# A recurrent attention layer with a sign-weight feed-forward gate on one core: where the dots of a block are summed, and where the last block's output weights are requested

## The chip, the cores and the metric

The kernel runs on one core of a Trainium2 chip. The metric is the device time of one execution in microseconds (us). The core has five engines that each work through their own instructions in order: PE (TensorE, matmuls), DVE (VectorE), ACT (ScalarE), POOL (GpSimd) and SP (SyncE). Here SP issues the plain transfers, and POOL issues those that add to what lies at the target. PSUM is the memory that TensorE writes; the kernel holds six rotating banks for matmul results ("mm") and one bank each for two running sums ("dots" and "squares").

## The reference, cut to what matters

All numbers are float32. x has 2048 tokens of 512 values. There are 16 heads of 128 channels, so 2048 channels.

```python
xn = layernorm(x)
q, k, v = (silu(xn @ W) for W in (Wq, Wk, Wv))     # 512 -> 2048 channels
z, a, b = xn @ Wz, xn @ Wa, xn @ Wb                # a, b: one value per head
q, k, v = (causal_dwconv4(u, w) for u, w in ...)   # 4 taps over the tokens
q, k = rotate(q), rotate(k); q, k = q / |q|, k / |k|    # per head
for s in range(4):                                  # lags 0..3
    attn = sum_over_head(q * lag(k, s)) / sqrt(128)
    out += attn * sigmoid(lag(a, s) * b) * lag(v, s)
out = out * rsqrt(mean(out * out)) * norm_w * silu(z)
s = out @ Wout                                      # 2048 -> 512
g = silu((relu(xn @ sign(up)) * up_scale) @ sign(down) * down_scale * output_scale)
return x + s * g
```

The "dots" are the sums of q times lagged k over each head's channels, for four lags: 16 heads x 4 lags x 2048 tokens.

## The kernel before, in words

**Blocks and pairs.** The tokens are worked on in four blocks of 512 (b = 0 to 3), and the channels in eight pairs of heads (p = 0 to 7), 256 channels each, which lie as two halves (j = 0, 1) of 128 partitions. `step(p, b)` (line 563) does for one pair the q and k work of block b+1 and the v, z and output work of block b, so that the block behind and the block ahead are interleaved. Steps with b = -1 do only the q and k work of block 0, with the feed-forward of block 0 between (lines 695 to 713). Steps with b = 0, 1, 2 follow (715 to 717), and after them a loop written out for the last block's v, z and output work (719 to 781). From line 789 on comes the feed-forward of blocks 1 to 3.

**q and k.** `queries` and `products` project a pair (eight matmuls of 128x512 each for q and k), convolve on ACT and DVE, and rotate (`turn`). `products` then multiplies q with lagged k on DVE: a tile `pr` of 128x2048 for half 0 and `pr1` for half 1, from a pool tag "pr" with two buffers. The halves have to be added. In block 0 (`not b`) DVE adds pr1 to pr for pairs 0 to 5, and an accumulating transfer of POOL does it for pairs 6 and 7 (lines 362 to 365). In the other blocks POOL does it for even pairs; an odd pair is formed with DVE adds and then gathered by four POOL transfers of 32 partitions into the tile of the even pair before it (lines 376 to 383), so that one tile holds two pairs.

**Dots.** An entry in `dots_due` says which tile has to be summed over partitions. `sum_dots` (line 405) takes one entry and issues four matmuls with a 32-column stationary (the trace shows each matmul of fp32 operands as two records, so eight records), one per lag, into the bank "dots". In blocks 1 to 3 there are four entries per block, each summed in the step two pairs later. In steps with p = 2, 4 and 6 `sum_dots` stands after the v projection and ahead of the output projection (lines 586 and 587); with p = 0 it is handed to `output_projections` as `midway`, which calls it after two of four chunks (lines 532 and 593).

**Norms and coefficients.** `sum_squares` sums q and k squares into the bank "squares"; `norms` copies half of them with ACT (line 432, the tile shares tag "rk" with the staging tile of `gate_products`, line 228, from which POOL sums into ab_dram), takes the root on ACT and the reciprocal on DVE. `coefficients` (line 453) multiplies dots, norms and gates and stores 128x512 coefficients to DRAM (co_dram).

**v, z and output.** `values` convolves v. `weighted` (line 484) loads the coefficient rows of a pair, spread over 64 partitions each, as tiles `bc` (two per pair, four transfers, three buffers), and forms o on DVE. `gated_output` multiplies o by norm_w and silu(z) into `oz`. After each odd pair `output_projection` (line 529) multiplies oz of two pairs with wo: four chunks `po` of 128 tokens, four matmuls each (32 records in all). The first matmuls of a chunk need the even pair's oz and wo, the others the odd pair's. ACT copies each po to `part`, and POOL adds it to s_dram.

**Weights.** `load` (line 250) requests 512 KB of wq, wk, wv or wz into a pool with three buffers. `weights_of_output` (line 471) requests wz and then wo (three buffers of its own) of a pair; `gates_of_output` (line 477) projects z.

**What sets the order.** TensorE, DVE and some POOL instructions keep the order in which the program is written (class `InOrder`, line 68). ACT, the other POOL instructions and SP are ordered by a scheduler from dependencies and priorities; SP's requests in the last block are kept in written order from line 720 on. A request whose buffer is not yet free waits at the head of SP's queue, and all later requests wait behind it.

**The last block.** Lines 721 to 732 request v of pairs 0 and 1 and z and wo of pair 0, finish norms and dots, and form the coefficients. In the loop from line 752, iteration p requests z and wo of pair p (`zs`, line 761), v of pair p+2 (line 764), and then, in `weighted` (line 769), the bc rows of pair p:

```python
        if 0 < p < NP:
            zs = weights_of_output(p, last)
            v = values(p, last, raw)
        if p + 2 < NP:
            load(vs, "v", p + 2, last)
```

Of the kernel before, what the change touches and what calls it, by code (L numbers as in the profile page):

```python
# [49 lines left out]
LAGS = 4  # L50
# [3 lines left out]
NP = H // 2  # L54
# [27 lines left out]
def recurrent_layer(ctx: ExitStack, tc: tile.TileContext, a: dict, out: bass.AP):  # L82
    nc = tc.nc
# [3 lines left out]
    loads = {"by": nc.sync}  # L87
# [5 lines left out]
    of_head = const.tile([P, NP, LW], F32, name="of_head")  # L93
# [3 lines left out]
    of_heads = const.tile([P, NP // 2, LW], F32, name="of_heads")  # L97
# [150 lines left out]
    weights = {}  # L248

    def load(pool, n, p, b):  # L250
        w = pool.tile([P, KC, 2 * P], F32, tag="w", name=f"w{n}{p}_{b}", bufs=3)
        loads["by"].dma_start(w, a[f"w{n}"][p])
        weights[n] = w
# [24 lines left out]
    def raw_of(pool, n, p, b, bufs=2):  # L278

        raw = with_halo(pool, f"r{n}", "raw", bufs, p, b)  # L280
        project(n, p, b, raw[:, :, HALO:])
        keep_halo(f"r{n}", raw, p, b)
        return raw
# [15 lines left out]
    banks = {}  # L299

    dots_due = []
# [26 lines left out]
    def products(p, b, q, between=None, beside_k=None):  # L328

        n = f"_{p}_{b}"  # L330
        load(qks, "k", p, b)
        q0 = q[:, LAGS - 1]
        k = with_halo(qks, "k", "k", 1, p, b)
        raw = raw_of(qks, "k", p, b)
        if p % 2 == 0:
            sum_squares()
        convolve(1, p, raw, k[:, :, HALO:])
        keep_halo("k", k, p, b)
        if between:
            between()  # L340
        turn(q)
        if beside_k:
            beside_k()

        sq = [qks.tile([P, 2, TB], F32, tag=f"sq{j}", name=f"sq{j}" + n, bufs=2 - j) for j in range(2)]
        for j in range(2):
            nc.scalar.activation(sq[j][:, 0], q0[:, j], AF.Square)
            nc.scalar.activation(sq[j][:, 1], k[:, j, HALO:], AF.Square)
        nc.gpsimd.dma_start(sq[0], sq[1], accum_op=ALU.add)
        squares_due.append((p, sq[0]))  # L350
        def product(to, j, lo, hi):

            k0 = k[:, j, lo : lo + TB]
            k_lags = bass.AP(k0.tensor, k0.offset, [k0.ap[0], [1, hi - lo], k0.ap[1]])
            dve.tensor_tensor(to, q[:, lo:hi, j, :], k_lags, ALU.mult)

        pr = qks.tile([P, LAGS, TB], F32, tag="pr", name="pr0" + n, bufs=2)
        product(pr, 0, 0, LAGS)
        if not b or p % 2 == 0:
            pr1 = qks.tile([P, LAGS, TB], F32, tag="pr", name="pr1" + n, bufs=2)  # L360
            product(pr1, 1, 0, LAGS)
            if b or p >= NP - 2:
                nc.gpsimd.dma_start(pr, pr1, accum_op=ALU.add)
            else:
                dve.tensor_tensor(pr, pr, pr1, ALU.add)
        else:
            for lo in range(0, LAGS, 2):
                half = qks.tile([P, 2, TB], F32, tag="half", name=f"half{lo}" + n, bufs=1)
                product(half, 1, lo, lo + 2)
                dve.tensor_tensor(pr[:, lo : lo + 2], pr[:, lo : lo + 2], half, ALU.add)  # L370
        if not b:
            dots_due.append([p, pr, of_head[:, p], p == NP - 1, True])
            return


        for h in range(0, P, D // 2):
            first, second = slice(h, h + D // 4), slice(h + D // 4, h + D // 2)
            if p % 2 == 0:
                nc.gpsimd.dma_start(pr[first], pr[second], accum_op=ALU.add)
            else:  # L380
                both = dots_due[-1][1]
                nc.gpsimd.dma_start(both[second], pr[first])
                nc.gpsimd.dma_start(both[second], pr[second], accum_op=ALU.add)
        if p % 2 == 0:
            dots_due.append([p, pr, of_heads[:, p // 2], p == NP - 2, False])
        else:
            dots_due[-1][-1] = True

    def add(to, s, heads, src, start, stop):

        rows = to[LW * s : LW * s + LW, :]
        pe.matmul(rows, heads, src, start=start, stop=stop, tile_position=(0, LW * s))
# [11 lines left out]

    def sum_dots():

        p, pr, heads, last, _ = dots_due.pop(0)
        if p == 0:
            banks["dots"] = sums.tile([P, TB], F32, tag="dots", name="dots")
        for s in range(LAGS):  # L410
            add(banks["dots"], s, heads, pr[:, LAGS - 1 - s, :], p == 0, last)

    def sums_of_o(b):

# [49 lines left out]
    def values(p, b, raw):  # L464

        v = with_halo(vs, "v", "v", 1, p, b)
        convolve(2, p, raw, v[:, :, HALO:])
        keep_halo("v", v, p, b)
        return v

    def weights_of_output(p, b):
        load(vs, "z", p, b)
        wo = vs.tile([P, 2, HID], F32, tag="wo", name=f"wo_{p}_{b}", bufs=3)
        nc.sync.dma_start(wo, a["wo"][p])
        return weights["z"], wo

    def gates_of_output(p, b, loaded=None):

        weights["z"], wo = loaded or weights_of_output(p, b)
        z = vs.tile([P, 2, TB], F32, tag="z", name=f"z_{p}_{b}", bufs=1)  # L480
        project("z", p, b, z)
        return z, wo

    def weighted(p, b, v):

# [67 lines left out]
    def output_projections(midway=None):  # L553
        if midway and not outputs_due:
            midway()
        while outputs_due:
            outputs_due.pop(0)(midway)
            midway = None
# [4 lines left out]
    def step(p, b, beside_q=None, beside_k=None):  # L563

        at = b >= 0
        change = p == 0 and at
        q = queries(p, b + 1)
        if beside_q:
            beside_q()
        if change and b:  # L570
            sum_squares()
            norms(b)
        due = bool(dots_due) and dots_due[0][-1]
        if change and not b:

            def beside_k():
                norms(b)
                norms_in_rows(b)

        products(p, b + 1, q, (lambda: norms_in_rows(b)) if change and b else None, beside_k)  # L580
        if p == NP - 1 and b + 2 < NTB:
            gate_products(b + 2)
        if at:
            load(vs, "v", p, b)
            raw = raw_of(vs, "v", p, b, 1)
        if due and not change:
            sum_dots()
        if first_due:
            first_due.pop()()
        if at:  # L590
            v = values(p, b, raw)

        output_projections(sum_dots if change else None)
        if change:
            coefficients(b)
        if at:
            z, wo = gates_of_output(p, b)
            out_of = lambda: gated_output(p, b, weighted(p, b, v), z, wo)
            if change:
                first_due.append(out_of)  # L600
            else:
                out_of()
        if p == 1 and at:
            gate(b + 1)
        if b + 2 < NTB:
            if p < TC:
                statistics(b + 2, p)
            if p == TC - 1:
                centre(b + 2)
            elif p == 5:  # L610
                divide(b + 2)
# [102 lines left out]
    vs = att.enter_context(tc.tile_pool(name="vs", bufs=1, side="right"))  # L714
# [4 lines left out]
    last = NTB - 1  # L719
# [1 line left out]
    load(vs, "v", 0, last)  # L721
    raw = raw_of(vs, "v", 0, last, 1)
    load(vs, "v", 1, last)
    zs = weights_of_output(0, last)
    sum_squares()
    norms(last)
    norms_in_rows(last)
    v = values(0, last, raw)
    raw = raw_of(vs, "v", 1, last, 1)
    sum_dots()  # L730
    coefficients(last)
    output_projections()
# [19 lines left out]
    for p in range(NP + 1):  # L752
        if 1 < p < NP:
            weights["v"] = v_weights.pop(p)
            raw = raw_of(vs, "v", p, last, 1)
        if p:
            z, wo = gates_of_output(p - 1, last, zs)
        if p % 2 == 1:
            output_projections()
        if 0 < p < NP:  # L760
            zs = weights_of_output(p, last)
            v = values(p, last, raw)
        if p + 2 < NP:
            load(vs, "v", p + 2, last)
            v_weights[p + 2] = weights["v"]
        if p:
            gated_output(p - 1, last, o, z, wo)
        if p < NP:
            o = weighted(p, last, v)

        if p < NP:
            some = slice(2 * p, 2 * p + 2)
            pool.dma_start(up[:, some], signs_dram["up"][:, some])
        else:
            pool.dma_start(first_down, signs_dram["down"][:, 0:NFD])
        if p == 4:
            xs = in_two_terms(ffw, tokens(1), "xs", 1, [P, KC, TB], "xs1")
# [11 lines left out]
    with tc.tile_pool(name="ff", bufs=1, side="right") as ff, tc.tile_pool(  # L789
# [48 lines left out]
        for b in range(1, NTB):  # L838
            pf = [pfs.tile([P, HID], F32, name=f"pf{c}") for c in range(TC)]
            for f in range(2, NFC + 2):  # L840
# [19 lines left out]
                _, df, terms = hids.pop(0)  # L860
# [88 lines left out]
```

## Time and profile before

| what | value |
|---|---|
| time, median of 3 runs | 1442.33 us (1441.13 to 1446.36) |
| time of the profiled execution | 1443.7 us |
| its span, first to last instruction | 1441.9 us |
| mean granted TensorE clock | 0.992 |
| TensorE busy | 1408.2 us, 98% of the span |
| DVE busy | 1207.8 us, 84% |
| ACT busy | 611.4 us, 42% |
| HBM read and written | 157.67 and 35.68 MB |

A row of the waits gives who waited (engine, tile), for what, the total in us, how often, and the longest. A row of a timeline gives start and length in us, engine, line, operation, output and inputs, the number of records, and in brackets the idle time before it with what ended it. Nearly all TensorE, DVE and SP work shows line 76, the wrapper that keeps the written order, so rows are told apart by their tiles: pq, pk, pv, pz are projections, po the output projection, dots the sums. In the answers of the chain a line gives start, length and what worked or was waited for.

### The profile page before, as it was taken

The page shows a single profiled execution, that of the slowest core. Times are in us where ns is not written, and L with a number is a line of the kernel's source. Part 1 is how long each engine was busy: PE and PEld are TensorE (multiplying, and loading weights), DVE is VectorE, ACT ScalarE, POOL GpSimd, SP SyncE. Part 2 cuts the span into 40 slices and gives each one's busy share as a digit, 9 for nine tenths or more (in the row PEclk, how much of TensorE's full clock was granted, in tenths as well). Part 3 has the DMA queues.
Part 4 walks back from the last instruction along what each step waited for, and adds up shares of the span by engine and source line. Part 5 has one row for each costly group of instructions (what it writes and reads, how often), then busy time and mean ns, then how long its engine had stood idle before and what let it go on. Part 6 is the DMA issues. An engine that isn't in the chain of part 4 may idle for free. (4 is left out here: it accounts for less than half of the span.)

```text
span 1441.9 us, 12588 instructions
## 1 busy us (share of the span) xinstructions
PE 1408.2 (98%) x3950; PEld 686.5 (48%) x3950; DVE 1207.8 (84%) x1362; ACT 611.4 (42%) x1181; POOL 232.4 (16%) x319
## 2 busy tenths in 40 slices
PE   9999998999999999999999999999999999799998
PEld 4555543444434444444344444444443444378886
DVE  6999988999999979999999799999896777346454
ACT  7476555444444534454444435444432332132122
POOL 2222121111212121212122201121211111100000
PEclk9999999999999999999999999999999999899999
DMA  9879598887988687878986888796749777662120
GB/s 330 253 192 214 138 234 189 222 209 178 203 199 191 137 194 223 202 179 194 212 193 137 190 211 199 169 216 169 166 94 230 198 196 170 149 223 93 35 88 29
DMA packets 102065, 261.30 MB, mean 181 GB/s; under 512 B 18864, under 2 KB 19376, under 8 KB 97392
## 3 DMA queue, kind: packets, MB, share of 16 engines
q0 software_dynamic: 33376, 106.99, 38.4%
q1 hardware_dynamic: 68624, 153.53, 35.4%
q8 instruction: 31, 0.51, 0.1%
q14 instruction: 34, 0.28, 0.1%
HBM read 157.67 MB, written 35.68 MB: 134 GB/s over the span
## 5 line engine op out<-in xcount | busy, mean ns | idle before, releaser
L76 PE MATMUL po<-wo,oz 128*128 128x512 f32 x512 | 230.5, 607 | 9.4 <-DVE oz L76 9.4
L76 PE MATMUL pv<-xnT,wv 128*128 128x512 f32 x512 | 226.5, 594 | 2.2 <-DMA wv<-in_wv_dram 2.2
L76 PE MATMUL pz<-xnT,wz 128*128 128x512 f32 x512 | 226.1, 594 | 0.7 <-DMA wz<-in_wz_dram 0.7
L76 PE MATMUL pq<-xnT,wq 128*128 128x512 f32 x512 | 226.0, 593 | 0.2 <-ACT xnT L177 0.2
L76 PE MATMUL pk<-xnT,wk 128*128 128x512 f32 x512 | 225.2, 592 | 0.0
L76 PEld LDWEIGHTS po<-wo,oz 128*128 128x128 f32 x512 | 97.9, 194 | 141.6 <-issue 109.7
L76 DVE SCALAR_TENSOR_TENSOR q<-rq,conv_w,q 128x512 f32<-128x512 f32 x192 | 141.4, 749 | 27.8 <-ACT q L288 23.2
L76 DVE SCALAR_TENSOR_TENSOR k<-rk,conv_w,k 128x512 f32<-128x512 f32 x192 | 142.3, 751 | 23.5 <-ACT k L288 19.0
L76 PEld LDWEIGHTS pv<-xnT,wv 128*128 128x128 f32 x512 | 95.6, 189 | 130.2 <-issue 121.6
L76 PEld LDWEIGHTS pz<-xnT,wz 128*128 128x128 f32 x512 | 96.7, 190 | 126.5 <-issue 123.6
L76 PEld LDWEIGHTS pq<-xnT,wq 128*128 128x128 f32 x512 | 96.0, 189 | 126.1 <-issue 118.5
L76 PEld LDWEIGHTS pk<-xnT,wk 128*128 128x128 f32 x512 | 96.6, 189 | 121.0 <-issue 115.6
L76 DVE SCALAR_TENSOR_TENSOR v<-rv,conv_w,v 128x512 f32<-128x512 f32 x192 | 141.3, 750 | 4.5
L76 DVE SCALAR_TENSOR_TENSOR q<-q,turns 128x1024 f32<-128x1024 f32 (+1 forms) x128 | 127.1, 1014 | 2.3
L76 DVE TENSOR_TENSOR o<-o,te 128x1024 f32<-128x1024 f32 x96 | 117.6, 1225 | 3.3
L76 DVE TENSOR_TENSOR pr<-q,k 128x2048 f32<-128x2048 f32 x52 | 117.3, 2287 | 0.9
L76 DVE TENSOR_TENSOR te<-v,bc 128x1024 f32<-128x1024 f32 x96 | 117.0, 1219 | 0.4 <-DMA bc<-co_dram 0.4
L647 ACT ACTIVATE hid<-ph,up_scale 128x512 f32<-128x512 f32 x64 | 43.7, 684 | 120.0 <-PE ph L76 118.8
L76 DVE CAST hid_hi<-hid 128x512 fp32r<-128x512 f32 x64 | 27.2, 425 | 69.9 <-ACT hid L647 69.9
L76 PE MATMUL ph<-xs_hi,up 128*128 128x512 f32 x192 | 76.4, 398 | 0.7 <-ACT so_sb L419 0.7
L276 ACT ACTIVATE rq<-pq 128x512 f32<-128x512 f32 x64 | 38.1, 595 | 90.7 <-PE pq L76 90.6
L76 PE MATMUL ph<-xs_lo,up 128*128 128x512 f32 x192 | 75.8, 395 | 0.0
(142 smaller groups left out, 1660.0 us busy)
## 6 DMA issues: line engine op xcount, KB each, us to landing
bc<-co_dram SPq DMA_DIRECT2D x128, 256.0 KB, 6.4
pr<-pr POOLq DMA_DIRECT2D x72, 256.0 KB, 5.9
wq<-in_wq_dram SPq DMA_DIRECT2D x32, 512.0 KB, 6.4
wk<-in_wk_dram SPq DMA_DIRECT2D x32, 512.0 KB, 6.2
sq<-sq POOLq DMA_DIRECT2D x32, 512.0 KB, 6.3
wv<-in_wv_dram SPq DMA_DIRECT2D x32, 512.0 KB, 6.5
wz<-in_wz_dram SPq DMA_DIRECT2D x32, 512.0 KB, 6.3
wo<-in_wo_dram SPq DMA_DIRECT2D x32, 512.0 KB, 6.0
```

The source lines that it names most:

```text
L76: return self.tc.keep_in_program_order(getattr(self.engine, op)(*args, **kwargs))
L276: nc.scalar.activation(to[:, j, :], pp, AF.Silu)
L647: nc.scalar.activation(hid, ph, AF.Relu, scale=up_scale[:, f : f + 1])
```

## The change

In block 0 DVE adds the halves of pair 6 too, and the halves of pair 7 are not added at all: `dots_due` now holds a list of tiles, and `sum_dots` goes through pr and pr1 of pair 7 with four matmuls each, all into the same bank. In the steps with p = 2, 4 and 6 `sum_dots` is handed to `output_projections` as `midway`, as it was with p = 0. In the last block wo is requested on its own (`load_wo`), after the bc rows of the same pair, and wo of pair 0 behind wv of pair 2, both ahead of the coefficient store.

```diff
-            if b or p >= NP - 2:
+            if b:
                 nc.gpsimd.dma_start(pr, pr1, accum_op=ALU.add)
-            else:
+            elif p < NP - 1:
                 dve.tensor_tensor(pr, pr, pr1, ALU.add)
...
-            dots_due.append([p, pr, of_head[:, p], p == NP - 1, True])
+            prs = [pr, pr1] if p == NP - 1 else [pr]
+            dots_due.append([p, prs, of_head[:, p], p == NP - 1, True])
...
-        for s in range(LAGS):
-            add(banks["dots"], s, heads, pr[:, LAGS - 1 - s, :], p == 0, last)
+        for pr in prs:
+            for s in range(LAGS):
+                src = pr[:, LAGS - 1 - s, :]
+                add(banks["dots"], s, heads, src, p == 0, last and pr is prs[-1])
...
-    def weights_of_output(p, b):
-        load(vs, "z", p, b)
+    def load_wo(p, b):
         wo = vs.tile([P, 2, HID], F32, tag="wo", name=f"wo_{p}_{b}", bufs=3)
-        nc.sync.dma_start(wo, a["wo"][p])
-        return weights["z"], wo
+        loads["by"].dma_start(wo, a["wo"][p])
+        return wo
...
-        if due and not change:
-            sum_dots()
         if first_due:
             first_due.pop()()
...
-        output_projections(sum_dots if change else None)
+        output_projections(sum_dots if due else None)
...
     load(vs, "v", 1, last)
-    zs = weights_of_output(0, last)
+    load(vs, "z", 0, last)
     sum_squares()
...
     raw = raw_of(vs, "v", 1, last, 1)
+    load(vs, "v", 2, last)
+    wo = load_wo(0, last)
     sum_dots()
     coefficients(last)
...
         if 0 < p < NP:
-            zs = weights_of_output(p, last)
+            load(vs, "z", p, last)
             v = values(p, last, raw)
+        if p and p + 2 < NP:
+            load(vs, "v", p + 2, last)
         if p + 2 < NP:
-            load(vs, "v", p + 2, last)
             v_weights[p + 2] = weights["v"]
...
             o = weighted(p, last, v)
+        if 0 < p < NP:
+            wo = load_wo(p, last)
```

In the steps, `gates_of_output` now only projects z; the requests of wz and wo stand in front of it in `step` in the same order as before.

More of the change, by code (lines that the diff above doesn't have):

```diff
@@ L380, in products @@
             else:
-                both = dots_due[-1][1]
+                both = dots_due[-1][1][0]
                 nc.gpsimd.dma_start(both[second], pr[first])
@@ L384, in products @@
         if p % 2 == 0:
-            dots_due.append([p, pr, of_heads[:, p // 2], p == NP - 2, False])
+            dots_due.append([p, [pr], of_heads[:, p // 2], p == NP - 2, False])
         else:
@@ L405, in sum_dots @@
     def sum_dots():
-        p, pr, heads, last, _ = dots_due.pop(0)
+        p, prs, heads, last, _ = dots_due.pop(0)
         if p == 0:
             banks["dots"] = sums.tile([P, TB], F32, tag="dots", name="dots")
-        for s in range(LAGS):
-            add(banks["dots"], s, heads, pr[:, LAGS - 1 - s, :], p == 0, last)
+        for pr in prs:
+            for s in range(LAGS):
+                src = pr[:, LAGS - 1 - s, :]
+                add(banks["dots"], s, heads, src, p == 0, last and pr is prs[-1])
     def sums_of_o(b):
@@ L469, in values, with gates_of_output @@
         return v
-    def weights_of_output(p, b):
-        load(vs, "z", p, b)
+    def load_wo(p, b):
         wo = vs.tile([P, 2, HID], F32, tag="wo", name=f"wo_{p}_{b}", bufs=3)
-        nc.sync.dma_start(wo, a["wo"][p])
-        return weights["z"], wo
-    def gates_of_output(p, b, loaded=None):
-        weights["z"], wo = loaded or weights_of_output(p, b)
+        loads["by"].dma_start(wo, a["wo"][p])
+        return wo
+    def gates_of_output(p, b):
         z = vs.tile([P, 2, TB], F32, tag="z", name=f"z_{p}_{b}", bufs=1)
         project("z", p, b, z)
-        return z, wo
+        return z
     def weighted(p, b, v):
@@ L596, in step @@
         if at:
-            z, wo = gates_of_output(p, b)
+            load(vs, "z", p, b)
+            wo = load_wo(p, b)
+            z = gates_of_output(p, b)
             out_of = lambda: gated_output(p, b, weighted(p, b, v), z, wo)
@@ L756, in recurrent_layer @@
         if p:
-            z, wo = gates_of_output(p - 1, last, zs)
+            z = gates_of_output(p - 1, last)
         if p % 2 == 1:
```

## The prediction

> **What bounds the kernel now.** I read the page's busy shares first, then TensorE's waits, then the timeline at each wait, then the chain that ended last.
>
> ```profile
> PE 1408.2 (98%) x3950; PEld 686.5 (48%) x3950; DVE 1207.8 (84%) x1362; ACT 611.4 (42%) x1181; POOL 232.4 (16%) x319
> ...
> PE po L76 <- DVE oz L76: 9.4, 5, 7.7
> PE dots L76 <- DMA pr<-pr: 7.6, 2, 4.3
> PE dots L76 <- issue: 3.2, 1, 3.2
> PE pv L76 <- DMA wv<-in_wv_dram: 2.2, 1, 2.2
> ```
>
> TensorE is busy for 98% and waits for about 27 us in all (total, times, longest). So only its waits and its pace can be won. Three of them are dots waiting for a sum of pr; the longest is po waiting for oz.
>
> ```profile
> 221.40 1.93 PE L76 MATMUL dots<-pr,of_head 128*32 128x512 f32 x8 [4.29 <-DMA pr<-pr]
> ...
> 283.48 12.28 PE L76 MATMUL po<-wo,oz 128*128 128x512 f32 x28 [0.28 <-DVE oz L76]
> ...
> 426.31 1.93 PE L76 MATMUL dots<-pr,of_heads 128*32 128x512 f32 x8 [3.34 <-DMA pr<-pr]
> 428.17 14.57 PE L76 MATMUL po<-wo,oz 128*128 128x512 f32 x32
> ...
> 575.91 12.28 PE L76 MATMUL po<-wo,oz 128*128 128x512 f32 x28 [0.68 <-DVE oz L76]
> ...
> 718.55 1.07 PE L76 MATMUL dots<-pr,of_heads 128*32 128x512 f32 x8 [3.15 <-issue]
> 719.56 15.64 PE L76 MATMUL po<-wo,oz 128*128 128x512 f32 x32
> ```
>
> TensorE's timeline at the places that the change touches (start, us, idle before). The wait at 718.55 is put down to "issue", but it stands where the one at 426 stood a block earlier and the instruction waits for the same four pr transfers, so I take it as the same wait. After each wait the pace is low for a while: 32 records of po take 13.74 elsewhere, 15.64 here.
>
> ```profile
> 1208.58 12.03 PE po L76 x28
> ...
> 1220.63 0.33 SPq L474
> ...
> 1222.03 10.86 DMA bc<-co_dram
> ...
> 1242.33 15.37 PE po L76 x28
> ```
>
> The chain in the last block: wo of pair 7 (L474) waits on SP until po of pair 5 has freed its buffer, the bc rows of pair 7 stand behind it, o starts when they land, and TensorE idles 7.70 us; the 28 records after it take 15.37 for 12.03.
>
> [...] 3.15 to 4.29 us of idling cost 1.6 to 1.9 more, 7.70 cost 3.3, 2.23 (at 1094) none. [...] from 200 to 216 us, with ten weight loads on SP, the DMA share is 1.00 and POOL's small ab_dram sums take 6 us each.
>
> **Part 1, first block's pairs 6 and 7.** Removed: two 1 MB accumulating transfers (median 9.4 us). Added: one DVE add of 128x2048 for pair 6, 2.29 us (its row at 158.64), and four more matmuls for pair 7, 8 records, 1.0 us on TensorE. The add is hidden by DVE's waits for ACT up to 204.6 (0.79, 0.70, 0.79, together 2.28); uncovered it would cost 2.3. TensorE reaches dots at 217.1, the second product of pair 7 is done at 203.8, so the 4.29 wait goes, with 1.6 of slow pace (dots 1.93 for 1.06, then 7.60 for 6.87), less 1.0: TensorE is 4.9 us ahead at pq (226.0 for 230.86).
>
> It meets oz of pair 1 next, which let it go on at 283.48 (wait 0.28). DVE has run since 222.67 with only two waits, for ACT's k multiply (0.71 and 1.21), and these go with an earlier pk: -1.9. Against that, in the built order of the changed kernel ACT's copy of the squares stands ahead of the second k multiply, no longer behind it:
>
> ```profile
> 211.36 0.72 ACT L288 ACTIVATE k<-rk,conv_w 128x512 f32<-128x512 f32 x1
> 215.63 0.58 ACT L432 COPY sq<-squares 64x512 f32<-64x512 f32 x1 [3.55 <-DMA ab_dram<-ab_sb]
> ...
> 222.67 3.35 DVE L76 RECIPROCAL r<-r 64x512 f32<-64x512 f32 x1 [3.21 <-ACT r L436]
> ```
>
> The copy waits for the last ab_dram sum. Nothing shows when that lands without the pr transfers beside it: by 211 (then nothing is late and the reciprocal comes 2.4 earlier) up to 215.6 as before (2.5 later). I take 215.0, since the weight loads that slow it stay: copy 0.58, kept row 0.2, k multiply 0.72 give 216.5; DVE's k half 2.33, turn 4.05, norm 1.09, ACT's root 0.63 give 224.6, or +1.9. That cancels the -1.9: oz comes when it did, TensorE idles some 6 us in front of it, pays 1.7 of slow pace again, and has the moved dots (next part) still to do. End of that po: 283.5 + 12.1 + 1.0 + 1.7 = 298.3 for 295.6. **Part 1 is given back: +2.7 here** (-3.3 to +3.3 by the two ends).
>
> **Part 2, dots between the halves.** At pairs 2, 4 and 6 of blocks 0 to 2 the four dots (1.0 us) move behind two of four po chunks, 6.9 us. No work is added.
> - Block 0, pair 6: TensorE comes at 423.0 + 2.7 = 425.7, oz is there (422.1), the sum lands by 426.3 for dots at 432.6. End 425.7 + 13.74 + 1.0 = 440.4 for 442.6 before: -2.2.
> - Block 1, pair 2: TensorE comes to the second oz 1.0 us sooner and waits 1.7 for 0.68, with dots still to do: +1.0, so -1.2. Too short for the slow pace.
> - Block 1, pair 6: comes at 715.4 - 1.2 = 714.2, ends 728.9 for 735.1: -6.2.
> - Block 2, pair 2 (wait 0.21 now): +1.0, so **-5.2**.
>
> DVE does not cap this between blocks: it waits 5.81, 1.58, 0.64 and 1.58 for ACT from 522 to 538, and 6.64, 1.48 and 1.83 from 814 to 828, so it follows an earlier TensorE. The pr buffer is kept 6.9 us longer; the tightest product that needs it starts 10.9 us after dots end (block 2, pair 6), so 4.0 are left.
>
> **Part 3, last block.** SP now sends wv of pair 2 and wo of pair 0 ahead of the coefficient store (1085.5 for 1088.9), and each further wo behind its own pair's bc rows.
> - wv lands about 1092, before pv at 1094.6: wait 2.23 gone. But wz of pair 1 still follows bc (1096.6, landing about 1104), and po waits for oz of pair 1 at 1127.6, a DVE chain from the landing of bc at 1099.22 without gaps. So the early waits (2.23, 0.66, 0.50) pay only what bc gains from 512 KB less behind the store: 0 to 2, taken as 0.7.
> - bc of pair 3 no longer waits for po (wo at 1138.2); bc of pair 7 goes at about 1195 to 1202, behind wz of pair 7 (freed by pz of pair 5 at 1194.9) and DVE's release of a bc buffer, and not at 1221.4. With 10.4 us to land (median here) o runs from about 1213 to 1222, z of pair 7 ends at 1229.8, oz at 1230.5. TensorE needs it at 1234.6. Gone: 7.70 and 15.37 - 12.03 = 3.3, **-11.0**.
> - Late next: wo of pair 7, still asked for at 1220.6; at 6 to 12 us it lands by 1233, needed at 1234.6. wz of pairs 4 and 6, behind wo of pairs 3 and 5, wait for later releases anyway (1146.8, 1188.0).
> - After po, the chain so, ss_dram, ss_acc, rms moves with po's end (1257.7 to 1269.5 before, TensorE's wait 0.23).
>
> Sum: -5.2 - 0.7 - 11.0 = **-16.9**. Span 1441.9 to 1425.0; the profiled run's 1443.7 to 1426.8; against the median of the runs, 1442.3, **1425.4**.
>
> **Rivals.**
> - A: the gain at 217 is kept, because the ab_dram sums land early once 2 MB of pr traffic is gone. Then oz of pair 1 is 4.3 earlier, TensorE idles under 3 us, +1.0 - 4.3 = -3.3 instead of +2.7: -22.9, 1419.4. For it: half of that traffic stood just ahead of these sums. Against: they are slowest under SP's ten loads.
> - B: in the last block another wait takes the place of bc: wo of pair 7 lands late or DVE comes late after bc of pair 6. Half of the 11.0 lost gives 1431, all of it 1436. Against: 4 us and more of room by the sums above.
> - C, slower: DVE stops for the pr buffer that dots now keep. From 4.0 us of delay beyond my sum the product waits at pair 6, soon at all nine places; 3 us at each are 27 us: 1452. Against: the other places have 7 us and more.
> - That the scheduler undoes the move is out: the built order has dots after two po chunks and wo behind bc.
>
> **How the numbers follow.** Main 0.60, A 0.22, B 0.13, C and the like 0.05. The range 1418 to 1433 takes in A and the milder half of B. A change under 0.5% (7.2 us) can't be told from none: B's far end lies there. Faster 0.94, same 0.03, slower 0.03.
>
> **What would show it.** Right: no wait of dots on pr; a wait of po for oz of 4 to 6 us near 280 with a low clock after it; 1 to 2 us of the same wait at pair 2 of blocks 1 and 2; no 7.7 us wait near 1215 to 1225, and full clock there. Wrong: an unbroken TensorE near 280 (A), po waiting for wo or oz in the last block (B), DVE products waiting for dots (C).

## The result and the profile after

| | before | after |
|---|---|---|
| time, median of 6 runs | 1441.66 us (1438.01 to 1446.36) | 1430.61 us (1428.79 to 1431.89) |
| time of the profiled execution | 1443.7 us | 1430.83 us |
| its span | 1441.9 us | 1429.0 us |
| mean granted TensorE clock | 0.992 | 0.995 |

The ratio is 0.9922, with a 95% interval of 0.9904 to 0.9941: about 11 us faster. The forecast was 1425.4 us (range 1418 to 1433), so the direction and the range held and the size was 5.2 us too large.

First the page's busy shares, then TensorE's waits in the kernel after:

```profile
PE 1405.1 (98%) x3958; PEld 686.0 (48%) x3958; DVE 1209.7 (85%) x1363; ACT 612.0 (43%) x1181; POOL 231.3 (16%) x317
...
PE po L76 <- DVE oz L76: 10.0, 3, 6.7
PE pz L76 <- DMA wz<-in_wz_dram: 3.2, 1, 3.2
```

The two rows of dots waiting for pr (7.6 and 3.2 us before) and that of wv are gone. In their place po waits 10.0 us in all for oz, 6.7 of it at one spot, and pz waits 3.2 for wz (0.7 before). The list has moved as much as it has shrunk. TensorE's timeline shows where:

```profile
283.58 8.08 PE L76 MATMUL po<-wo,oz 128*128 128x512 f32 x12 [6.75 <-DVE oz L76]
291.59 1.07 PE L76 MATMUL dots<-pr,of_heads 128*32 128x512 f32 x8
...
863.31 5.42 PE L76 MATMUL po<-wo,oz 128*128 128x512 f32 x12 [1.39 <-DVE oz L76]
...
1101.21 8.80 PE L76 MATMUL pz<-xnT,wz 128*128 128x512 f32 x16 [3.18 <-DMA wz<-in_wz_dram]
...
1230.35 13.89 PE L76 MATMUL po<-wo,oz 128*128 128x512 f32 x32
```

The last line is part 3: the 32 records of the last projection run unbroken. In the kernel before, 28 of them took 15.36 us behind a wait of 7.70:

```profile
1242.33 15.36 PE L76 MATMUL po<-wo,oz 128*128 128x512 f32 x28 [7.70 <-DVE oz L76]
```

On SP, in the kernel after, the bc rows of pair 7 go out at 1192.89 (1221.38 before), ahead of wo of pair 7:

```profile
1192.89 4.60 SPq L76 DMA_DIRECT2D bc<-co_dram  x4
1218.21 0.33 SPq L76 DMA_DIRECT2D wo<-in_wo_dram  x1
```

The first line of TensorE's timeline is part 1 given back: 12 records take 8.08 us where they take 5.42 at 863.31.

The chain to that wait on ACT and DVE, in the kernel after:

```profile
210.75 0.58 ACT L276 ACTIVATE rk<-pk 128x512 f32<-128x512 f32 x1
215.51 0.58 ACT L436 COPY sq<-squares 64x512 f32<-64x512 f32 x1 [4.18 <-DMA ab_dram<-ab_sb]
216.10 0.72 ACT L288 ACTIVATE k<-rk,conv_w 128x512 f32<-128x512 f32 x1
...
216.85 2.33 DVE L76 SCALAR_TENSOR_TENSOR k<-rk,conv_w,k 128x512 f32<-128x512 f32 x3 [4.95 <-ACT k L288]
...
224.88 3.35 DVE L76 RECIPROCAL r<-r 64x512 f32<-64x512 f32 x1 [0.70 <-ACT r L440]
```

ACT's copy of the squares waits for the last ab_dram sum, the k multiply stands behind it, DVE waits 4.95 us for that, and the reciprocal comes at 224.88 for 222.67 before. From there to oz of pair 1 DVE works without a gap, so each us that the copy is late comes through to oz. po goes on at 283.58, as in the kernel before (283.48), though TensorE now stands in front of it some 5 us sooner.

To place the gains I compare the start of the same pz in both traces (after minus before, us):

| pz that starts (before) at | after minus before | the prediction's running sum |
|---|---|---|
| 251.5, behind pair 7's dots | -5.2 | -4.9 |
| 295.6, behind po of block 0, pair 2 | +4.0 | +2.7 |
| 442.6, block 0, pair 6 | -0.9 | -2.2 |
| 588.0, block 1, pair 2 | +0.3 | -1.2 |
| 735.0, block 1, pair 6 | -4.6 | -6.2 |
| 880.0, block 2, pair 2 | -3.4 | -5.2 |
| 1146.6, behind po of pair 1, last block | -2.4 | -5.9 |
| (ph behind the last po, 1259.4) | -13.4 | -16.9 |
| (end of the span, 1441.9) | -12.9 | -16.9 |

### The profile page after: what moved, and what is told of

Read it like the earlier page. It is cut to its first block, busy times and chain, and to the rows that moved or that the text cites. A ratio compares the mean times of both kernels' runs of the same rounds, so it can differ in the third digit from the quotient of the medians.

```text
span 1429.0 us, 12596 instructions
## 1 busy us (share of the span) xinstructions
PE 1405.1 (98%) x3958; PEld 686.0 (48%) x3958; DVE 1209.7 (85%) x1363; ACT 612.0 (43%) x1181; POOL 231.3 (16%) x317
## 4 chain that ended last, share of the span: by engine, by line
PE 63%; DVE 22%; issue 6%; DMA 3%; ACT 3%; SPq 1%; POOL 0%; DVEq 0%; POOLq 0%; ACTq 0%
PE po L76 13%; PE pz L76 11%; PE pv L76 9%; PE pq L76 8%; PE pk L76 8%; PE pf L76 6%; PE ph L76 6%; DVE q L76 5%; DVE pr L76 3%; DVE k L76 3%; DVE o L76 3%; DVE te L76 2%; DVE v L76 2%; DVE half L76 1%; PE dots L76 1%
## 5 line engine op out<-in xcount | busy, mean ns | idle before, releaser
L547 ACT COPY part<-po 128x512 f32<-128x512 f32 x64 | 37.1, 580 | 84.8 <-PE po L76 49.5
```

What stands on the lines that cost most here:

```text
L547: nc.scalar.copy(part, po)
```

## The experiments

The theory after the traces: part 3 is the gain; part 2 works as forecast but pays 1 us or more at pair 2; part 1 loses, because ACT's copy delays the oz on which po then waits. The kernels were timed in three groups, each beside the kernel before on the same chip (medians there 1440.96, 1441.39 and 1442.33 us), so the medians of the groups differ by up to 1.4 us for the same kernel. The changed kernel itself was timed beside the kernel before only in the result above. A difference from it is therefore one between chips: I give it by the medians, and, where it matters, also by the two ratios to the kernel before.

### The parts one by one

**Part 1 alone**: the kernel before with these lines of the change and those that make `sum_dots` go through a list of tiles.

```diff
-            if b or p >= NP - 2:
+            if b:
                 nc.gpsimd.dma_start(pr, pr1, accum_op=ALU.add)
-            else:
+            elif p < NP - 1:
                 dve.tensor_tensor(pr, pr, pr1, ALU.add)
...
+            prs = [pr, pr1] if p == NP - 1 else [pr]
```

> The kernel before with part 1 alone (pairs 6 and 7 of the first block). Theory (given back): no wait of dots at 217, but a wait of po for oz of pair 1 of 5 to 7 us near 281 with a low clock after it, so that the pz after it starts 2 to 4 us later than the 295.6 of before; the wait of 3.34 for pr at 426 then shrinks, and the whole is between 2 us faster and 2 us slower than before, 1440 to 1444. Rival (the gain at 217 is kept, and after's wait near 280 comes from the dots between the halves): po is unbroken near 281 and the whole is 4 to 5 us faster, about 1437.

Measured: 1439.38 us, ratio 0.999 (0.9969 to 1.001). TensorE's timeline in it:

```profile
282.82 14.36 PE L76 MATMUL po<-wo,oz 128*128 128x512 f32 x28 [4.91 <-DVE oz L76]
...
428.06 1.94 PE L76 MATMUL dots<-pr,of_heads 128*32 128x512 f32 x8 [3.18 <-DMA ss<-o]
```

The wait at 217 is gone and comes back at 278, with dots still ahead of po; so the return does not come from the move of dots. The pz behind it starts 1.4 us later than before (I had said 2 to 4). Wrong was that the wait at 426 would shrink: it is 3.18 and only starts later. (The row names ss, not pr, as what ended it; what these dots read is still pr.) By the time, part 1 alone makes no difference that can be told.

**Part 2 alone**: the kernel before with

```diff
-        if due and not change:
-            sum_dots()
...
-        output_projections(sum_dots if change else None)
+        output_projections(sum_dots if due else None)
```

> The kernel before with part 2 alone (dots between the halves). Theory: two waits of 3.34 and 3.15 with their slow pace go, 4.8 and 4.9 us; at pair 2 of blocks 0, 1 and 2 the dots come after the wait for oz and no longer inside it, 1.0 to 1.2 us each; the wait of 4.29 at 221 stays. Sum -9.7 + 3.4 = -6.3, about 1435. Rival (part 2 costs nothing at pair 2, and what was lost there in after comes from part 1): 9 to 10 us faster, about 1432.

Measured: 1439.66 us, ratio 0.9993 (0.9981 to 1.0005): 1.0 us faster, between 2.7 faster and 0.7 slower. My -6.3 is refuted by the time, and so is the rival's -9 to -10. The trace was taken a second time with the kernel before likewise (below); it shows the steps as forecast, and a part of what is missing.

**Part 3 alone**: the changed kernel with parts 1 and 2 undone.

> The kernel before with part 3 alone (requests in the last block). Theory: the 7.70 us wait near 1234 and 3.3 of slow pace go (11.0), wv's 2.23 goes, wz of pair 1 makes a wait of about 3 us near 1104 with 1.9 of slow pace, 0.3 to 0.5 more at the tail: 9 to 10 us faster, about 1432. Rival (the stall at wz of pair 1 in after is there because TensorE came 3.4 us earlier; alone there is next to none): 11.5 to 13 us faster, about 1429.

Measured: 1430.59 us, ratio 0.9928 (0.9909 to 0.9947): 10.4 us faster. Its timeline has the wait for wz of pair 1, and then 8.55 us for 16 records that take 7.03 elsewhere:

```profile
1104.32 8.55 PE L76 MATMUL pz<-xnT,wz 128*128 128x512 f32 x16 [3.29 <-DMA wz<-in_wz_dram]
```

TensorE starts the last block's first pz here only 0.4 us before the kernel before (1087.03 for 1087.43), and is earlier at wz (1101.03 for 1103.90) only by part 3's own removal of the wait for wv. So the wait does not need parts 1 and 2, and the rival is out. This is also the time of the whole change (1430.61): on top of part 3, parts 1 and 2 together bring nothing that the medians show.

**Parts 2 and 3**: the changed kernel with part 1 undone.

> The changed kernel with part 1 undone (parts 2 and 3 alone). Theory (part 1 costs more than it brings): the wait of 4.29 for pr at 221 is back, the wait for oz near 281 is under 1.5 us at full clock, and it is about 3 us faster than the changed kernel: some 1427.5 on its median of 1430.6. Rival (part 1 pays as its own removed wait says, 4.9): 4 to 5 us slower than the changed kernel, about 1435.

Measured: 1429.29 us, ratio 0.9913 (0.9892 to 0.9934), 1.3 us under the changed kernel. The rival (part 1 pays 4.9) is out; the theory's 3 us is more than the time shows. In the trace the pz behind po of pair 2 starts at 296.99 for 299.56 with part 1, so 2.6 us there are the price of part 1 (2.2 against the second trace of the changed kernel, 299.14).

### What returns part 1

**A buffer of its own for the copy of the squares.** In the changed kernel the copy's tile shares its buffer with the tile that the ab_dram sums read. One word is changed:

```diff
-        sq2 = qks.tile([P, TB], F32, tag="rk", name=f"sq2{b}", bufs=1)[0 : 2 * LW]
+        sq2 = qks.tile([P, TB], F32, tag="sq2", name=f"sq2{b}", bufs=1)[0 : 2 * LW]
```

> The changed kernel with a buffer of its own for the copy of the squares, so that ACT's copy no longer waits for the last ab_dram sum. Theory (that copy, ahead of the second k multiply, is what returns part 1): the copy runs at about 211.3 without its wait of 4.18, DVE's k half about 4 us earlier, the reciprocal near 221 (224.88 in the changed kernel), oz of pair 1 near 279.5, po waits about 2.5 us for 6.75 and keeps its pace; pz after it starts 6 to 7 us earlier than in the changed kernel, and most of that stays to the end: about 1424.5 for 1430.6. Rival (oz of pair 1 is set by something else, such as DVE's own work or the rq and rk rows): the wait near 280 stays over 5 us, the time within 2 us of the changed kernel.

Measured: 1425.42 us, ratio 0.9896 (0.9871 to 0.9921), 5.2 us under the changed kernel by the medians, 3.7 by the ratios. All six runs (1423.62 to 1427.96) lie below every run of the changed kernel (1428.79 to 1431.89). ACT, DVE and TensorE in its timeline:

```profile
212.20 0.58 ACT L436 COPY sq<-squares 64x512 f32<-64x512 f32 x1
...
221.57 3.35 DVE L76 RECIPROCAL r<-r 64x512 f32<-64x512 f32 x1 [0.70 <-ACT r L440]
...
280.28 5.42 PE L76 MATMUL po<-wo,oz 128*128 128x512 f32 x12 [2.61 <-DVE oz L76]
```

The links moved as forecast, by a little less than the 4 us that I gave: no wait ahead of the copy, the reciprocal 3.3 us sooner, po 3.3 us sooner, 2.61 us of wait for 6.75 and full pace behind it. The next pz starts at 293.59 for 299.56. The traces of the two kernels show the same order of work on DVE, POOL and SP, and on ACT around the copy, so the wait for the shared buffer is the cause of what part 1 gave back. It takes the copy's place ahead of the second k multiply too: in the kernel before the same wait (3.55 us) stood behind that multiply and cost nothing there. Putting the multiply ahead again was not tried.

**Part 1 undone in the best kernel.** The kernel with this buffer and the next edit, with part 1 taken out again:

> The changed kernel with the buffer for the copy of the squares and the dots of pair 2 ahead of the projection, but with part 1 undone. Theory (part 1 pays once the copy no longer delays DVE): the wait of 4 to 5 us of dots for pr at 221 is back, with up to 1.9 of slow pace after it; oz of pair 1 is then no longer waited for near 280 (1.41 us with part 1), so 3 to 5 us slower than with part 1 (1419.4): about 1423.5. Rival (part 1 is worth nothing in any order): within 1.5 us of 1419.4.

Measured: 1425.92 us against 1419.39 with part 1, so part 1 is worth 6.5 us there by the medians of two groups, 5.5 by the ratios (0.9888 and 0.985), more than the 3 to 5 that I gave. The profiled execution was the slowest run (1429.42): TensorE waited 5.50 us for wz of pair 1 in it, for 4.13 with part 1; whether that comes from part 1 is not shown. By the trace alone, ahead of that wait, part 1 is worth 4.2 us (the pz behind po of block 1, pair 6 starts at 722.50 with it, 726.69 without).

### What part 2 pays at pair 2

**Dots of pair 2 ahead of the projection again**, those of pairs 4 and 6 as in the change:

```diff
+        if due and at and p == 2:
+            sum_dots()
+            due = False
         if first_due:
             first_due.pop()()
```

> The changed kernel with the dots of pair 2 back ahead of the projection in blocks 0 to 2 (pairs 4 and 6 stay between the halves). Theory: at pair 2 the dots (1.0 us) fill part of a wait for oz that is there anyway, so each block gives 1.0 to 1.2 back, and in blocks 1 and 2 the wait (1.86 and 1.39) falls under 0.9: 3 us in all, about 1427.5. Rival (the sum of pair 0's pr is late there too, and the dots would wait): a wait of dots for pr of 1 us and more at pair 2, and no gain.

Measured: 1424.68 us, ratio 0.9894 (0.9869 to 0.9918), 5.9 us under the changed kernel by the medians, 4.0 by the ratios, for 3 expected. Its timeline:

```profile
282.74 13.96 PE L76 MATMUL po<-wo,oz 128*128 128x512 f32 x28 [4.56 <-DVE oz L76]
...
571.99 12.28 PE L76 MATMUL po<-wo,oz 128*128 128x512 f32 x28 [0.67 <-DVE oz L76]
```

In blocks 1 and 2 the next pz starts 1.2 us sooner each, as forecast. In block 0 it is 2.5 and not 1.0: the shorter wait is followed by 1.7 us of slow pace (13.96 for 12.28) where the longer one had 2.7 (8.08 for 5.42). Against the second trace of the changed kernel it is 1.8, so a part of these 2.5 is one execution's. The dots at pair 2 idled once, for 0.60 us in block 0, which is under the rival's 1 us, and the gain is there, so the rival is out.

**Both edits together**:

> The changed kernel with both edits: own buffer for the copy of the squares, dots of pair 2 ahead of the projection. Theory: the two gains add, 6 to 7 and 3, less 0.5 since the dots near 280 then fill a wait of 2.5 us: about 1422, waits for oz near 280 under 1.6 us. Rival (the last block's waits are pinned to transfers and take a part of any earlier gain): 1425 to 1428, with longer waits than 3.2 us for wz or po after 1090.

Measured: 1419.39 us (1418.03 to 1422.93), ratio 0.985 (0.9824 to 0.9876): 22.0 us under the kernel before, 11.2 under the changed one (10.4 by the ratios). By the medians the two gains add (5.2 + 5.9). This beats both kernels, by two small edits.

```profile
280.66 12.28 PE L76 MATMUL po<-wo,oz 128*128 128x512 f32 x28 [1.41 <-DVE oz L76]
...
1093.02 9.45 PE L76 MATMUL pz<-xnT,wz 128*128 128x512 f32 x16 [4.13 <-DMA wz<-in_wz_dram]
```

The time leaves the rival out, but it has a point: TensorE starts the pz of pair 0 of the last block 9.1 us earlier than in the changed kernel, waits 4.13 us for wz of pair 1 and keeps 7.5 of them. (The profiled execution was the slowest of the six, 1422.93 us.)

### The wait for wz of pair 1

**wz of pair 1 requested early**, in the place of wo of pair 0:

```diff
     load(vs, "v", 2, last)
-    wo = load_wo(0, last)
+    wz0 = weights["z"]
+    load(vs, "z", 1, last)
+    wz1, weights["z"] = weights["z"], wz0
...
-        if 0 < p < NP:
+        if p < NP:
             wo = load_wo(p, last)
```

> The changed kernel with wz of pair 1 of the last block requested where wo of pair 0 is (ahead of the coefficient store), and wo of pair 0 behind the bc rows of pair 0. Theory (oz of pair 1 is next): the wait of 3.18 for wz and its 1.9 of slow pace go, TensorE reaches po about 5 us earlier and waits there about 4 us for oz of pair 1, which comes at 124.4 after 1000 as in the changed kernel: 0 to 1 us gained, 1429.5 to 1430.6, more lost where the new wait brings its own slow pace. Rival (the wait for wz was a loss by itself): 4 to 5 us faster, about 1426.

Measured: 1430.48 us, ratio 0.9941 (0.9917 to 0.9965): the changed kernel's time by the medians, 2.7 us slower by the ratios. TensorE in its timeline:

```profile
1123.85 12.28 PE L76 MATMUL po<-wo,oz 128*128 128x512 f32 x28 [1.50 <-DVE oz L76]
```

The wait for wz is gone, and po waits for oz of pair 1, as the theory said. The wait is 1.50 and not 4, since TensorE came 2.0 us later to the last block in this execution (1086.02 for 1084.03), which the wait for oz then absorbed. Behind po the pz starts at 1142.83, for 1144.19 and 1143.07 in the two traces of the changed kernel: a wait of 3 us with its slow pace is gone, and 0.2 to 1.4 us are won in the traces, nothing in the medians. A wait that is taken away ahead of a later one on another engine's chain was worth little here. (Whether it pays on the best kernel, where wz costs more, wasn't tried.)

### Second traces of the same kernels

**The kernel before, part 2 alone and the changed kernel once more**, unchanged, to see what varies:

> The kernel before once more, for a second trace of it. Theory (a stall of a given length brings the slow pace in one execution and not in another): the waits of dots at 221, 426 and 718 are again 2.4 to 5 us, but at least one of the three, or of wv's at 1094, has another slow pace after it than in the first trace (0.9, 0.9 and 1.9 us there; none for wv), and the time moves by 1 to 4 us with it. Rival (the slow pace follows the length of the wait alone): the same three figures within 0.3 us where the waits agree within 0.5.

> Part 2 alone once more, for a second trace. Theory: the wait of 1.86 for oz at pair 2 of the second block is there again to 0.05 us, its slow pace (1.7 us in the first trace of this kernel, none in that of the changed kernel) may be there or not. Rival: it is 1.7 again, being set by the order of this kernel's instructions.

> The changed kernel once more, for a second trace. Theory: waits of 6.75, 1.86, 1.39 and about 3.2 us again within 1 us; the slow pace after the one of 1.86 (none in the first trace) may be 1.7. Rival (slow pace follows from the kernel's order): none after 1.86, 2.9 after 6.75 and 1.9 after 3.2, each to 0.3 us.

Measured: 1441.51, 1439.4 and 1429.67 us in the profiled executions, one each. The waits are there again, most of them within 1 us; the pace behind them is not the same. The wait of the second block, pair 2, in the two traces of part 2 alone (first, then second):

```profile
572.22 7.11 PE L76 MATMUL po<-wo,oz 128*128 128x512 f32 x12 [1.86 <-DVE oz L76]
```

```profile
573.36 5.42 PE L76 MATMUL po<-wo,oz 128*128 128x512 f32 x12 [1.85 <-DVE oz L76]
```

The same wait, the same order of work, and 1.7 us of slow pace or none. Over seven traces with this wait (1.85 to 1.87 us) three have it (part 2 alone, parts 2 and 3, early wz), four have not (part 2's second trace, both of the changed kernel, the buffer for the copy). The kernel before, in its second trace:

```profile
1095.68 8.80 PE L76 MATMUL pv<-xnT,wv 128*128 128x512 f32 x16 [2.44 <-DMA wv<-in_wv_dram]
...
1240.82 13.74 PE L76 MATMUL po<-wo,oz 128*128 128x512 f32 x28 [7.27 <-DVE oz L76]
```

wv's wait of 2.44 brings 1.7 (8.80 for 7.11 in the first trace, after 2.23), and the long wait of the last block 1.5 where it brought 3.1 in the first (15.36, full pace 12.28). In the changed kernel's second trace a wait of 6.90 brings 1.8 (7.23 for 5.42), where 6.75 brought 2.7. So the rivals, that the slow pace follows from the wait's length alone or from the order of the kernel, are out. Where the low pace goes on into the next row of the timeline, these figures are a lower bound. What decides whether it comes is not shown.

**What stays open of part 2.** Comparing the second traces, part 2's own steps make it 6.2 us faster up to 1083, as forecast (4.4 and 5.3 won at the pairs 6, three times 1.2 paid). But this execution had lost 2.4 by 251, where the two kernels do the same (TensorE came 1.0 later to the dots of pair 7, and waited 1.3 longer for pr), and lost 2.4 more between 1083 and the end, where wz of pair 1 and the last stall wait longer for a TensorE that comes earlier. So a part of its gain is taken back by the last block as long as part 3 isn't there. That doesn't explain why the medians also show only 1.3 us on top of part 3; how much of this is the spread of single runs (7.5 to 17 us from lowest to highest in that group) is not settled.

## Why the prediction was right or wrong

**Right.** What bounds the kernel, and part 3's last stall: "-11.0" was forecast, and the stretch from the last pz to ph behind the last po is 11.0 us shorter in the trace. That it agrees so closely is luck: between the second traces of the two kernels the same stretch is 9.0 shorter. The term itself was 10.8, since the 12.03 in "15.37 - 12.03" is a row of the chain that ends where SP takes over, and 28 records at full pace take 12.28. bc of pair 7 went out at 1192.89 (forecast 1195 to 1202) and wo of pair 7, requested at 1218.21, was not late, so B is out. Part 3 alone carries the result. That part 1 "is given back" was right with its mechanism: the copy at 215.51 (the sum's landing was taken as 215.0), the reciprocal +2.2 for +1.9, po resumed at 283.58 for 283.5. The buffer experiment shows it. Rival A (the sums land early) is out by the 4.18 us wait of the copy, and C by DVE, which waits nowhere for dots. Of part 2 the steps in the trace were right: -4.8 and -4.9 at the pairs 6, +1.2 twice. (A reading of the prediction that its argument does not need is off: SP's timeline before shows eight weight loads between 199.76 and 209.07, not ten, and the last of the three small ab_dram sums took 3 us, not 6.)

**Wrong, by the terms of the sum.** Between the two profiled executions the forecast was 16.9, measured 12.9. The 4.0 are:

- "pays 1.7 of slow pace again" behind the wait near 280: 2.7 in this trace (1.8 in the second), so that po ends +4.0 for +2.7. Cost 1.3. The slow pace came as forecast, but its size was taken from waits of 3.15 to 4.29 us. Over 280 to 284, 284 to 288 and 288 to 292 us the granted clock was 0.77, 0.50 and 0.88 in the first trace and 0.61, 0.54 and 1.00 in the second. The wait ended at 283.58 and 284.01, so more of the low clock fell on work in the first.
- Part 2's steps at pair 2: +1.2 for +1.0 each, and rounding: 0.5. "Too short for the slow pace" failed as a rule: it held in both traces of the changed kernel (5.42 us for 12 records behind 1.86 us), not in three others (7.11 or 7.12).
- "So the early waits pay only what bc gains ... taken as 0.7": -0.7 forecast, +1.0 measured, cost 1.7. The wait of 2.23 for wv went as forecast, but TensorE then came to wz of pair 1, which SP issued at 1092.49 behind the first bc rows, waited 3.18 us and ran at low pace for 1.8 more. I had named wz as following bc and put no wait on it. That oz of pair 1 is the bound behind it was right, as the early wz shows: with this wait cured, po waits for oz and the time is no better.
- The feed-forward behind the last po gave back 0.5 (13.4 to 12.9), which I had at nothing. From its ph to the end of the span the fourteen traces take 182.4 to 183.2 us, so it lies within their spread; it has no cause that is shown.

The last 1.2 of the 5.2 lie in the base: the first profiled execution of the kernel before stood 1.4 us above its three runs' median (2.0 above six), that of the kernel after only 0.2 above its own. The forecast took 16.9 out of an execution whose stalls were dearer than usual; its last stall brought 3.1 us of slow pace, where the second trace has 1.5 and the two of part 2 alone 1.5 and 1.9.

**Failed beyond the sum.** Taking part 2 as 5 to 6 us of time: the runs show about 1. The trace's differences were right and still did not come out in the medians.

## What to carry to other kernels

When a wait goes, look at once for what the same engine meets next, and whether that waits on a chain that the edit leaves alone or makes longer: here a copy on ACT held up by a shared buffer cost part 1 its gain, and a tag of its own for one tile gave 3.7 to 5.2 us. Work moved off a spot should leave filler where another wait stands anyway: dots in front of an oz that is late cost nothing, behind it they cost 1.2 us (blocks 1 and 2). Price a TensorE stall as its length plus a slow pace that can differ from execution to execution: behind the same wait of 1.86 us it was 0 or 1.7 us here (5.42 or 7.11 us for 12 records), and none followed the waits of 1.39, 1.41 and 1.50 us above (5.42 us for 12 records, 12.28 for 28). Take a second trace before a term of 3 us is drawn from one.

## What the runs showed of the hardware

The slow pace behind a stall does not follow from its length alone. The same wait of 1.86 us cost 1.7 more in three traces of seven (7.11 us for 12 records of po) and nothing in four (5.42); waits of 1.94, 2.00 and 2.44 us on wv brought 1.7 (8.80 for 7.11), while 2.04 and 2.23 brought none of it; a stall of 7 to 9 us in the last block brought 3.1 once and 1.5 to 1.9 in four other traces. The wait for wv in the two traces of part 2 alone (first, then second):

```profile
1092.12 7.11 PE L76 MATMUL pv<-xnT,wv 128*128 128x512 f32 x16 [2.04 <-DMA wv<-in_wv_dram]
```

```profile
1091.52 8.80 PE L76 MATMUL pv<-xnT,wv 128*128 128x512 f32 x16 [2.00 <-DMA wv<-in_wv_dram]
```

The granted clock was low where the pace was slow. The rows below give from and to, length, busy time of TensorE and then of the other engines, and the granted clock as the third figure from the end. In the kernel before, where the stall of the last block ended at 1242.33 after 7.70 us and 28 records then took 15.36:

```profile
1240.00:1244.00 4.00, 1.67 (x2) 0.84 (x3) 3.83 (x7) 1.06 (x1) 1.19 (x3) 0.50 0.00 0
1244.00:1248.00 4.00, 4.00 (x6) 1.69 (x5) 1.03 (x3) 0.58 (x1) 1.86 (x3) 0.50 0.98 192
1248.00:1252.00 4.00, 4.00 (x10) 1.62 (x9) 0.00 (x0) 0.58 (x1) 0.21 (x1) 0.93 1.07 335
```

In its second trace, where the stall ended at 1240.82 after 7.27 us and they took 13.74:

```profile
1240.00:1244.00 4.00, 3.18 (x4) 1.49 (x5) 3.47 (x6) 1.01 (x1) 2.17 (x3) 0.53 0.35 66
1244.00:1248.00 4.00, 4.00 (x11) 1.75 (x10) 0.00 (x0) 0.81 (x2) 0.89 (x1) 1.00 1.08 260
```

By these rows the clock was low for some 6 us behind the first stall and for some 3 behind the second. What decides how long it stays low, and whether the pace falls at all behind a wait of about 2 us, is not shown: no run was made to move a stall in time and leave the rest as it was.
